# Quantised silu rows of places 3 and 0: absolute value and rounding placed behind the next step's first exponentials; modulations projected ahead of the down product

## The chip, the cores and the metric

The kernel runs on one core of a Trainium2 chip. The time is that of one execution on the device, in microseconds (us); the median of the runs is what is compared. Engines are named as the profile names them: PE is TensorE (matmul, with PEld its weight loads), DVE is VectorE, ACT is ScalarE, POOL is GpSimd, SP is SyncE, which here only issues DMAs.

## The reference

The input x has 16 batches of 512 rows of 256 numbers. Per batch:

```
xn = layernorm(x)
# attention block, 16 heads
q, k   = xn @ cq_w, xn @ ck_w                 # 8 columns a head
qm, km = xn @ qmod_w + b, xn @ kmod_w + b     # the modulations: one number per row and head
scores = causal_kernel(pooled xn)[i - j] + qm[i] + km[j] + 0.15 q.k / sqrt(8),  causal
attn   = softmax(scores);  ctx = attn @ (xn @ v_w + v_b)
h = layernorm(xn + ctx @ out_w + out_b);  s = layernorm(h + gelu(h @ ffn_w1 + b) @ ffn_w2 + b)
# gate block, inputs and weights rounded to FP4 (blocks of 16, E2M1 grid)
hid = silu(fp4(xn) @ fp4(w_gate).T) * (fp4(xn) @ fp4(w_up).T)     # 704 wide
g   = silu(fp4(hid) @ fp4(w_down).T)
out = x + s * g
```

`fp4(t)` divides each block of 16 by its scale (its largest absolute value / 6), rounds to 0, 0.5, 1, 1.5, 2, 3, 4, 6 and multiplies by the scale again. "silu's rows" are the rows of `hid`, which the kernel quantises this way before the product with `w_down` (the down product).

## The kernel before, in words

Everything is laid out as 64 steps: 16 batches times 4 places, g = 0 to 3. Step (b, g) does the attention of heads 4g to 4g + 3 of batch b, and the gate block of the row tile t = g (128 of 512 rows) of batch b. In the same steps the remainder of the batch before (`old` = b - 1) is finished: its output projection in places 0 and 1, its feed-forward block (the contractions `f`) in places 2 and 3. The projections of the batch after (q, k, the modulations m, v) are made by `coming`, partly in places 3, 0 and 1.

A step begins with `context` (32 matmuls into the tile cp: the exponentials of the step before times v), and ct, a copy of cp on ACT. Then the main loop works through a string of letters, `PLAN[g]`:

- W: one burst of scores (PE, tile ws, a pair of PSUM banks with one buffer), their exponential (ACT, tile pr) and POOL's product of that with a table (`tabled`, L560).
- M: the same scores for the *next* step (PE, tile ms, two of six common banks), and `!`: their row maxima (DVE, tile junk, result mx). `!` also runs `caught_up()`, which does deferred work: the low halves of the split projections and their DMAs.
- c: a piece of `coming`; l: a piece of the output projection; x: the turning of quantised inputs xq (PE xqtp, ACT xqT); y: the turning of the quantised hidden rows of the step before (PE hqtp, ACT hqT); k: the copy ct in place 1.

After the letters come the two halves of the hidden rows (PE gp/up/gu, ACT Silu, DVE product into the tile `wide`), the quantisation's first stages, and the down product of the tile of the step before (`gate`: 12 matmuls dp, then ACT Silu into `gated`). `expect(AF.Exp)` loads ACT's table for exponentials and `operands` issues the loads of qT and kT for the step after next (SP, L466 and L467).

The quantisation is a generator, `fp4_stages`, advanced with `next`: DVE finds the largest value amax of each block and its inverse inv, POOL makes the scale (L224) and scales the rows (L222); then ACT writes the scaled absolute value m (the tile m, bf16), DVE does two SCALAR_TENSOR_TENSOR instructions (max with m and add, max and subtract), which round, and POOL multiplies by the scale (L242). With `by_act=False` (in `fp4`, for weights) VectorE took the exponent bits with an AND on 32-bit integers instead, into a float32 tile, and needed two TENSOR_TENSOR behind it.

In the order of PE, DVE and ACT nothing is left to a planner: they execute in the order in which the code issues. POOL's instructions and SP's DMAs are ordered by the framework's scheduler by readiness. In the step before place 0 and place 1 (places 3 and 0), `next(stages)` near the end of the step issues the Abs, and `for _ in stages` at the end of the step the two roundings and L242, so that these come ahead of the next step's first letters on ACT and DVE.

The modulations are written by `split_m`: an Identity on ACT makes the high half, and a deferred `rest` the low half on DVE and four DMAs to q_d or k_d (L393).

Of the kernel before, what the change touches and what calls it, by code (L numbers as in the profile page):

```python
# [11 lines left out]

F32 = mybir.dt.float32
I32 = mybir.dt.int32
F32R = mybir.dt.float32r
BF16 = mybir.dt.bfloat16
AF = mybir.ActivationFunctionType
# [24 lines left out]

ROUND = 12582912.0
TURN = 6.283185
LEVEL = 6291456.0
POWER = 4194304.0
EXPONENT = 0x7F800000
UNDER = 1.0 + 2.0**-22


# [1 line left out]
def tile_block(ctx: ExitStack, tc: tile.TileContext, a: dict, pos: bass.AP, win: bass.AP, out: bass.AP):  # L52
# [140 lines left out]

    v_aug = [keep.tile([P, NT * H * VS + SLOT - VS], F32, name=f"va{i}", tag=f"va{i}") for i in range(2)]

    def fp4_stages(dst, src, n, width, by_act=True):

        nb = width // 16
        widest = 2 * D if width <= 2 * D else I_FF

        def temporary(name, columns):
            return sb.tile([P, widest // columns], F32, name=f"{name}{widest}", tag=f"{name}{widest}")[
                :n, : width // columns
            ]
# [12 lines left out]
        nc.gpsimd.tensor_tensor(blocks(dst), blocks(src), per_block(inv), ALU.mult)  # L222
        if by_act:
            nc.gpsimd.tensor_scalar(scale, amax, -1.0 / 6.0, -1e-12, ALU.mult, ALU.min)  # L224
            yield
            m = sb.tile([P, I_FF], BF16, name="m", tag="m")[:n, :width]
            act.activation(m, dst, AF.Abs, scale=POWER)
            yield
            dve.scalar_tensor_tensor(dst, m, 1.25 * POWER, dst, ALU.max, ALU.add)
            yield  # L230
            dve.scalar_tensor_tensor(dst, m, 1.25 * POWER, dst, ALU.max, ALU.subtract)
        else:
            nc.gpsimd.tensor_scalar(scale, amax, 1.0 / 6.0, 1e-12, ALU.mult, ALU.max)
            yield
            m = sb.tile([P, I_FF], F32, name="m32", tag="pr2")[:n, :width]
            dve.tensor_scalar(m.bitcast(I32), dst.bitcast(I32), EXPONENT, None, ALU.bitwise_and)
            dve.tensor_scalar(m, m, 1.0, LEVEL, ALU.max, ALU.mult)
            yield
            dve.tensor_tensor(dst, dst, m, ALU.add)
            yield  # L240
            dve.tensor_tensor(dst, dst, m, ALU.subtract)
        nc.gpsimd.tensor_tensor(blocks(dst), blocks(dst), per_block(scale), ALU.mult)  # L242

    def fp4(dst, src, n, width):
        for _ in fp4_stages(dst, src, n, width, False):
            pass


# [30 lines left out]
        for image, at in ((q_d[i], own + 2), (k_d[i], own), (k_d[i], own + 4)):  # L279
            nc.sync.dma_start(out=image[:, at : at + 2, :], in_=units)  # L280
    xns, vas, gates = {}, {}, {}
    later = []

    def caught_up():
        while later:
            later.pop(0)()

# [49 lines left out]
    def project(b, x):  # L337
# [44 lines left out]
        def split_m(acc, both, flip, image, at, p0):  # L382
            hi, lo = both[:, 0, :], both[:, 1, :]
            step = slice(None, None, -1) if flip else slice(None)
            act.activation(hi[:, step], acc[:, :P], AF.Identity, bias=m_bias)

            def rest():
                dve.scalar_tensor_tensor(
                    lo[:, step], acc[:, :P], m_bias, hi[:, step].bitcast(F32), ALU.add, ALU.subtract
                )  # L390
                for t in range(NT):
                    to = (NT - 1 - t if flip else t) * P
                    nc.sync.dma_start(  # L393
                        out=image[:, at : at + 2, to : to + P],
                        in_=both[2 * H * t + p0 : 2 * H * t + p0 + H, :, :].bitcast(F32),
                    )

            later.append(rest)
# [315 lines left out]

    HI = I_FF // 2

    def quantised(b, t):

        xq = sb.tile([P, 2, D], F32, name=f"xq_{b}_{t}", tag="xq", bufs=2)
        src = xns[b][t // 2].rearrange("p t d -> p (t d)")  # L720
        return xq, fp4_stages(xq.rearrange("p t d -> p (t d)"), src, P, 2 * D)

    def turned_x(b, t, xq, halves=False):
        xq = xq[:, t % 2, :]
        if halves:
            xqTs[b, t] = sb.tile([P, D], F32, name=f"xqT_{b}_{t}", tag="xqT")
            by_halves(f"xqtp_{b}_{t}", xqTs[b, t], [xq[:, c * P : (c + 1) * P] for c in range(NC)])
            yield 0.21
            return
        tp = bank(f"xqtp_{b}_{t}")  # L730
        for c in range(NC):
            turn(tp[:, c * P : (c + 1) * P], xq[:, c * P : (c + 1) * P])
        xqTs[b, t] = sb.tile([P, D], F32, name=f"xqT_{b}_{t}", tag="xqT")
        act.copy(xqTs[b, t], tp[:, :D])
        yield 0.21

    def hidden(b, t, xqT):

        hid = wide[t % 2]

        def halves():
            for s in range(2):
                cut = slice(s * HI, (s + 1) * HI)
                if s == 1:
                    both = ps_s.tile([P, 2, S], F32, name=f"gu_{b}_{t}", tag="ws")
# [12 lines left out]
                sl = sb.tile([P, HI], F32, name=f"sl_{b}_{t}_{s}", tag="sl", bufs=2)  # L758
                act.activation(sl, gp[:, :HI], AF.Silu)
                dve.tensor_tensor(hid[:, cut], up[:, :HI], sl, ALU.mult)  # L760
                yield

        return hid, halves(), fp4_stages(hid[:, :I_FF], hid[:, :I_FF], P, I_FF)

    def turned_hidden(b, t, hq, halves=False):
        hqT = sb.tile([P, NI, P], F32, name=f"hqT_{b}_{t}", tag="hqT")
# [20 lines left out]
    def expect(function):  # L787
# [8 lines left out]
        ("p|x||yytt|tt", ""),  # L796
    )
    PLAN = (
        "WM!lM!xWcclWM!llWcM!cWllM!y",
        "WM!lkxM!WcclWM!llWccM!llWM!hyy",  # L800
        "WM!fffxM!fWffM!ffhM!ffWffM!fWfffWyy",
        "WM!fffxM!fWiffM!ffWfM!iffWffM!fWffyy",
    )
# [408 lines left out]
    for s in range(STEPS):  # L1212
# [194 lines left out]
```

## Time and profile before

| what | value |
|---|---|
| runs, median (lowest to highest) | 1917.15 us (1915.87 to 1920.88), 3 runs |
| the profiled execution | 1914.35 us, span 1912.6 us |
| busy: PE, DVE, POOL, ACT | 91%, 72%, 68%, 59% of the span |
| mean granted clock of TensorE | 0.94 |
| place 0, steps of batches 2 to 15 | 345.65 us for 14, mean 24.69 |
| place 1, steps of batches 1 to 15 | 482.43 us for 15, mean 32.16 |

The span is cut by the start of `context` into steps. The busy share is an average; a wait counts where TensorE stands still, and the profile names the instruction that ended it. Matmul rows with "x8" are several instructions taken together, and the number behind it in square brackets is the idle time before the row and what ended it. The granted clock is that of TensorE as a share of full speed; while it is 0.5, matmuls take twice as long.

### The profile page before, as it was taken

How to read it: one execution, taken by the hardware profiler on the slowest of the kernel's cores; microseconds unless marked ns; L12 is line 12 of the kernel's file. 1: busy time of each engine (PE TensorE's matmuls, PEld its weight loads, DVE VectorE, ACT ScalarE, POOL GpSimd, SP SyncE). 2: the span in 40 equal slices, each digit the busy share in tenths (PEclk: the TensorE clock that was granted, in tenths of full speed). 3: DMA queues.
4: the chain of work that ended last, by engine and by line, in shares of the span. 5: the costliest groups of instructions: out<-in, count | busy, mean ns of one | idle time of the engine just before them, and what ended most of it. 6: DMA issues, size and time to landing. Idle time of an engine off the chain costs nothing.

```text
span 1912.6 us, 35681 instructions
## 1 busy us (share of the span) xinstructions
PE 1748.2 (91%) x12473; PEld 1276.1 (67%) x12473; DVE 1376.7 (72%) x3736; ACT 1121.6 (59%) x1906; POOL 1304.8 (68%) x1112
## 2 busy tenths in 40 slices
PE   5769799899999989899999989899999989999998
PEld 2234467676776767686777767676776767677666
DVE  5767567877686877778686777877687777777654
ACT  5655456566565656566565656656565656565552
POOL 4467466768586876768585876768586776768571
PEclk8868699999999999999999999999998999998999
DMA  6254242414233242414233242413333242322200
GB/s 201 79 156 129 66 135 72 139 55 125 80 104 118 71 125 73 135 51 127 85 104 118 69 125 75 135 51 113 99 104 114 70 124 79 111 63 89 65 21 12
DMA packets 127223, 184.93 MB, mean 97 GB/s; under 512 B 15410, under 2 KB 57844, under 8 KB 127044
## 3 DMA queue, kind: packets, MB, share of 16 engines
q1 hardware_dynamic: 122544, 181.25, 30.4%
q8 instruction: 99, 1.62, 0.3%
q10 hardware_dynamic: 4052, 0.98, 0.3%
q14 instruction: 80, 0.66, 0.1%
q0 software_dynamic: 448, 0.42, 0.1%
HBM read 136.45 MB, written 45.09 MB: 95 GB/s over the span
## 4 chain that ended last, share of the span: by engine, by line
PE 61%; DVE 16%; ACT 5%; DMA 5%; issue 2%; POOL 1%; SPq 1%; DVEq 0%; ACTq 0%; POOLq 0%
PE f L73 22%; PE dp L73 5%; PE gu L73 5%; PE ws L73 4%; DVE xn L73 4%; PE ms L73 4%; DMA kT<-k_d 4%; PE op L73 4%; DVE junk L73 4%; PE cp L73 4%; PE gp L73 2%; PE up L73 2%; DVE xq L73 2%; PE qk_wq L73 2%; PE vp L73 2%
## 5 line engine op out<-in xcount | busy, mean ns | idle before, releaser
L560 POOL TENSOR_TENSOR pr<-pr,table 128x1024 f32<-128x1024 f32 (+2 forms) x448 | 768.4, 1743 | 124.7 <-ACT pr L73 124.3
L73 DVE CUSTOM_DVE_ANT_0 junk<-ms,mask 128x512 bf16<-128x512 f32 (+3 forms) x1024 | 501.7, 490 | 242.8 <-PE ms L73 173.0
L73 ACT ACTIVATE pr<-ws 128x1024 f32<-128x1024 f32 x320 | 327.7, 1024 | 149.6 <-PE ws L73 148.2
L73 PE MATMUL f<-w,act 64*128 64x256 f32 (+1 forms) x1984 | 282.5, 382 | 0.0
L73 DVE SCALAR_TENSOR_TENSOR wide<-m,wide 128x704 f32<-128x704 bf16 x130 | 131.2, 1010 | 157.1 <-ACT m L73 154.8
L73 ACT ACT_TABLE_LOAD x168 | 215.5, 1283 | 34.9 <-PE gp L73 17.2
L73 PE MATMUL f<-hT,w 128*128 128x256 f32 x1024 | 226.3, 379 | 0.0
L73 PE MATMUL ms<-kT,qT 36*128 36x512 f32 (+3 forms) x1024 | 205.4, 393 | 17.4 <-DMA kT<-k_d 15.7
L242 POOL TENSOR_TENSOR wide<-wide,scale 128x704 f32<-128x704 f32 (+1 forms) x71 | 96.3, 1356 | 177.5 <-DVE wide L73 174.6
L73 PE MATMUL ws<-qT,kT 38*128 38x512 f32 (+3 forms) x1024 | 195.6, 421 | 22.3 <-ACT pr L73 11.4
L73 PEld LDWEIGHTS f<-hT,w 128*128 128x128 f32 x1024 | 194.5, 190 | 26.7 <-ACT hT L73 0.3
L73 PEld LDWEIGHTS f<-w,act 64*128 64x128 f32 (+1 forms) x1984 | 192.3, 186 | 17.1
L73 PE MATMUL dp<-wdT,hqT 128*128 128x256 f32 x768 | 177.4, 381 | 0.0
L73 PEld LDWEIGHTS dp<-wdT,hqT 128*128 128x128 f32 x768 | 145.7, 191 | 27.0
L73 PEld LDWEIGHTS ws<-qT,kT 38*128 38x128 f32 x1024 | 107.1, 205 | 67.5 <-issue 22.9
L73 PE MATMUL cp<-pr,va 128*32 128x512 f32 (+3 forms) x2048 | 151.9, 435 | 0.0
L73 PEld LDWEIGHTS ms<-kT,qT 36*128 36x128 f32 x1024 | 122.2, 204 | 44.4 <-issue 13.7
L73 ACT ACTIVATE act<-f,fb 128x256 f32<-128x256 f32 x256 | 114.8, 471 | 51.0 <-PE f L73 49.2
L73 PEld LDWEIGHTS cp<-pr,va 128*32 128x32 f32 x2048 | 62.1, 110 | 89.7 <-issue 75.0
L222 POOL TENSOR_TENSOR wide<-wide,inv 128x704 f32<-128x704 f32 (+1 forms) x71 | 105.6, 1488 | 23.7 <-DVE inv L73 23.6
L224 POOL TENSOR_SCALAR scale<-amax 128x32 f32<-128x32 f32 (+1 forms) x98 | 39.2, 400 | 109.0 <-DVE amax L73 106.2
L73 ACT ACTIVATE sl<-gu 128x352 f32<-128x352 f32 x64 | 29.6, 463 | 119.1 <-PE gu L73 119.0
(218 smaller groups left out, 3199.0 us busy)
## 6 DMA issues: line engine op xcount, KB each, us to landing
table<-rv SPq DMA_DIRECT2D x64, 1024.0 KB
kT<-k_d SPq DMA_DIRECT2D x256, 76.0 KB
qT<-q_d SPq DMA_DIRECT2D x256, 72.0 KB
x<-in_L_attn_x_dram SPq DMA_DIRECT2D x21, 512.0 KB
q_d<-q_hi SPq DMA_DIRECT2D x32, 256.0 KB
q_d<-q_lo SPq DMA_DIRECT2D x32, 256.0 KB
k_d<-k_hi SPq DMA_DIRECT2D x32, 256.0 KB
k_d<-k_lo SPq DMA_DIRECT2D x32, 256.0 KB
```

Of the source, the lines that this page charges most:

```text
L73: return lambda *args, **kw: self.follow(op(*args, **kw))
L222: nc.gpsimd.tensor_tensor(blocks(dst), blocks(src), per_block(inv), ALU.mult)
L224: nc.gpsimd.tensor_scalar(scale, amax, -1.0 / 6.0, -1e-12, ALU.mult, ALU.min)
L242: nc.gpsimd.tensor_tensor(blocks(dst), blocks(dst), per_block(scale), ALU.mult)
L560: nc.gpsimd.tensor_tensor(part, part, table[:, mine, j * P :], ALU.mult)
```

## The change

Four things:

1. In `fp4_stages` the Abs on ACT is now only chosen with `by_act=True`; the other way makes the same bf16 tile m on DVE (an AND with 0x7FFF on the high 16 bits of each float, then a multiply), and both ways share the two rounding instructions. `by_act` is set for the hidden rows of batches b > 0 and for inputs when there is an `old` batch; in batch 0 and for the weights DVE does it.
2. `PLAN` of places 0 and 1 gets the letters a and z. a advances the stages of the step before by one: the Abs, on ACT behind the first W (in place 1 behind k as well). z does the rest, the two roundings and POOL's L242, behind the second `!`. At the end of places 0 and 3 the stages are left open. x moves behind the second W and its c's.
3. At the end of place 0 the modulations (`coming`, one piece: 16 matmuls qk_m, the two Identities, the two low halves) come ahead of the down product instead of behind it.
4. The DMAs of `split_m` are put in a list `sending` and issued by a `caught_up()` with `send`; `caught_up(False)`, used for the modulations at the end of place 0, leaves them for the next one.

```
-    def fp4_stages(dst, src, n, width, by_act=True):
+    def fp4_stages(dst, src, n, width, by_act=False):
...
+        nc.gpsimd.tensor_scalar(scale, amax, -1.0 / 6.0, -1e-12, ALU.mult, ALU.min)
+        yield
+        m = sb.tile([P, I_FF], BF16, name="m", tag="m")[:n, :width]
         if by_act:
-            nc.gpsimd.tensor_scalar(scale, amax, -1.0 / 6.0, -1e-12, ALU.mult, ALU.min)
-            yield
-            m = sb.tile([P, I_FF], BF16, name="m", tag="m")[:n, :width]
             act.activation(m, dst, AF.Abs, scale=POWER)
-            yield
-            dve.scalar_tensor_tensor(dst, m, 1.25 * POWER, dst, ALU.max, ALU.add)
-            yield
-            dve.scalar_tensor_tensor(dst, m, 1.25 * POWER, dst, ALU.max, ALU.subtract)
         else:
-            nc.gpsimd.tensor_scalar(scale, amax, 1.0 / 6.0, 1e-12, ALU.mult, ALU.max)
-            yield
-            m = sb.tile([P, I_FF], F32, name="m32", tag="pr2")[:n, :width]
-            dve.tensor_scalar(m.bitcast(I32), dst.bitcast(I32), EXPONENT, None, ALU.bitwise_and)
-            dve.tensor_scalar(m, m, 1.0, LEVEL, ALU.max, ALU.mult)
-            yield
-            dve.tensor_tensor(dst, dst, m, ALU.add)
-            yield
-            dve.tensor_tensor(dst, dst, m, ALU.subtract)
+            dve.tensor_scalar(m.bitcast(I16), dst.bitcast(I16)[:, 1::2], 0x7FFF, None, ALU.bitwise_and)
+            dve.tensor_scalar(m, m, POWER, None, ALU.mult)
+        yield
+        dve.scalar_tensor_tensor(dst, m, 1.25 * POWER, dst, ALU.max, ALU.add)
+        yield
+        dve.scalar_tensor_tensor(dst, m, 1.25 * POWER, dst, ALU.max, ALU.subtract)
         nc.gpsimd.tensor_tensor(blocks(dst), blocks(dst), per_block(scale), ALU.mult)
...
-    later = []
-
-    def caught_up():
+    later, sending = [], []
+
+    def caught_up(send=True):
         while later:
             later.pop(0)()
+        while send and sending:
+            sending.pop(0)()
+
+    def whole(pieces):
+        for _ in pieces:
+            pass
+        yield
...
                 dve.scalar_tensor_tensor(
                     lo[:, step], acc[:, :P], m_bias, hi[:, step].bitcast(F32), ALU.add, ALU.subtract
                 )
+                sending.append(send)
+
+            def send():
                 for t in range(NT):
...
-    def quantised(b, t):
+    def quantised(b, t, by_act=False):
...
-        return hid, halves(), fp4_stages(hid[:, :I_FF], hid[:, :I_FF], P, I_FF)
+        return hid, halves(), fp4_stages(hid[:, :I_FF], hid[:, :I_FF], P, I_FF, b > 0)
...
     PLAN = (
-        "WM!lM!xWcclWM!llWcM!cWllM!y",
-        "WM!lkxM!WcclWM!llWccM!llWM!hyy",
+        "WMa!lM!zWccxlWM!llWcM!cWllM!y",
+        "WMka!lM!zWccxlWM!llWccM!llWM!hyy",
...
+                "a": stages,
+                "z": whole(stages),
...
-            xqs[(4 * pair[0] + pair[1]) // 2], more = quantised(*pair)
+            xqs[(4 * pair[0] + pair[1]) // 2], more = quantised(*pair, has_old)
...
+        if has_old and g == 0:
+            for _ in take(coming, 1):
+                caught_up(False)
         if gating:
             gate(*gating, hqTs.pop(gating))
-        if has_old and g == 0:
-            next(coming, None)
         if has_old and g in (1, 2):
             acts[g - 1] = expand(old, g - 1, turned_hs[g - 1], stages)
-        if not has_old or g % 3 == 0:
-            next(stages, None)
...
         if s + 2 < STEPS:
             ahead = operands(*divmod(s + 2, H // 4))
-        for _ in stages:
-            pass
+        if g in (1, 2) or not following:
+            for _ in stages:
+                pass
```

More of the change, by code (lines that the diff above doesn't have):

```diff
@@ L13 @@
 F32 = mybir.dt.float32
-I32 = mybir.dt.int32
+I16 = mybir.dt.int16
 F32R = mybir.dt.float32r
@@ L44 @@
 TURN = 6.283185
-LEVEL = 6291456.0
 POWER = 4194304.0
-EXPONENT = 0x7F800000
 UNDER = 1.0 + 2.0**-22
@@ L222, in fp4_stages @@
         nc.gpsimd.tensor_tensor(blocks(dst), blocks(src), per_block(inv), ALU.mult)
+        nc.gpsimd.tensor_scalar(scale, amax, -1.0 / 6.0, -1e-12, ALU.mult, ALU.min)
+        yield
+        m = sb.tile([P, I_FF], BF16, name="m", tag="m")[:n, :width]
         if by_act:
-            nc.gpsimd.tensor_scalar(scale, amax, -1.0 / 6.0, -1e-12, ALU.mult, ALU.min)
-            yield
-            m = sb.tile([P, I_FF], BF16, name="m", tag="m")[:n, :width]
             act.activation(m, dst, AF.Abs, scale=POWER)
-            yield
-            dve.scalar_tensor_tensor(dst, m, 1.25 * POWER, dst, ALU.max, ALU.add)
-            yield
-            dve.scalar_tensor_tensor(dst, m, 1.25 * POWER, dst, ALU.max, ALU.subtract)
-        else:
-            nc.gpsimd.tensor_scalar(scale, amax, 1.0 / 6.0, 1e-12, ALU.mult, ALU.max)
-            yield
-            m = sb.tile([P, I_FF], F32, name="m32", tag="pr2")[:n, :width]
-            dve.tensor_scalar(m.bitcast(I32), dst.bitcast(I32), EXPONENT, None, ALU.bitwise_and)
-            dve.tensor_scalar(m, m, 1.0, LEVEL, ALU.max, ALU.mult)
-            yield
-            dve.tensor_tensor(dst, dst, m, ALU.add)
-            yield
-            dve.tensor_tensor(dst, dst, m, ALU.subtract)
+        else:
+            dve.tensor_scalar(m.bitcast(I16), dst.bitcast(I16)[:, 1::2], 0x7FFF, None, ALU.bitwise_and)
[4 more added lines that the diff above has]
+        dve.scalar_tensor_tensor(dst, m, 1.25 * POWER, dst, ALU.max, ALU.subtract)
         nc.gpsimd.tensor_tensor(blocks(dst), blocks(dst), per_block(scale), ALU.mult)
     def fp4(dst, src, n, width):
-        for _ in fp4_stages(dst, src, n, width, False):
+        for _ in fp4_stages(dst, src, n, width):
             pass
@@ L715, in tile_block @@
     HI = I_FF // 2
-    def quantised(b, t):
+    def quantised(b, t, by_act=False):
         xq = sb.tile([P, 2, D], F32, name=f"xq_{b}_{t}", tag="xq", bufs=2)
         src = xns[b][t // 2].rearrange("p t d -> p (t d)")
-        return xq, fp4_stages(xq.rearrange("p t d -> p (t d)"), src, P, 2 * D)
+        return xq, fp4_stages(xq.rearrange("p t d -> p (t d)"), src, P, 2 * D, by_act)
     def turned_x(b, t, xq, halves=False):
```

## The prediction

> **What bounds the kernel now.** I read the page first, then the waits of TensorE, then a table of windows, one per step of a place, then the timelines of one step in place 0 (batch 9, from 1103.60 us) and of the start of some steps in place 1. On the page TensorE (PE) has by far the largest share:
>
> ```profile
> PE 1748.2 (91%) x12473; PEld 1276.1 (67%) x12473; DVE 1376.7 (72%) x3736; ACT 1121.6 (59%) x1906; POOL 1304.8 (68%) x1112
> ```
>
> So time can be won only in TensorE's 164 us of idleness or in the stretches where its clock is halved. In the steady state its waits are at the start of the steps of places 0 and 1, and there are none in places 2 and 3. These are the large ones (engine, tile, releaser: us, times, longest):
>
> ```profile
> PE xqtp L73 <- ACT pr L73: 31.4, 15, 2.7
> PE ctp L73 <- ACT ct L73: 22.4, 15, 3.2
> PE ms L73 <- DMA kT<-k_d: 15.7, 24, 5.1
> ```
>
> The first two come from ScalarE (ACT), which does the absolute value, the table load, the copy ct and the first exponential in this order (start, duration):
>
> ```profile
> 1105.26 0.79 ACT L73 ACTIVATE m<-wide 128x704 bf16<-128x704 f32 x1 [1.18 <-DVE xq L73]
> 1106.07 1.28 ACT L73 ACT_TABLE_LOAD   x1
> 1107.47 0.57 ACT L73 COPY ct<-cp 128x512 f32<-128x512 f32 x1
> 1107.94 1.03 ACT L73 ACTIVATE pr<-ws 128x1024 f32<-128x1024 f32 x1
> ```
>
> The change attacks that chain. What decides is what comes next in the same step, on VectorE (DVE) and POOL:
>
> ```profile
> 1106.09 2.28 DVE L73 SCALAR_TENSOR_TENSOR wide<-m,wide 128x704 f32<-128x704 bf16 x2 [0.94 <-ACT m L73]
> 1108.29 0.68 DVE L73 CUSTOM_DVE_ANT_0 junk<-ms,mask 128x512 bf16<-128x512 f32 x1
> ...
> 1113.06 0.56 DVE L73 CUSTOM_DVE_ANT_0 junk<-ms,mask 128x384 bf16<-128x384 f32 x1 [0.54 <-PE ms L73]
> ```
>
> ```profile
> 1114.77 0.62 PEld L73 LDWEIGHTS ms<-kT,qT 36*128 36x128 f32 x4 [0.24 <-DVE mx L73]
> ```
>
> The reader sees VectorE go from the two rounding instructions through the first two pairs of maxima without a pause, and the fourth set of products for maxima (ms) waiting until the third maxima have been read: two banks of qk, two of op and two of ms fill the six. TensorE thus runs at the pace of VectorE at 1114.77, and for the 12.5 us to the step's end (1127.32) it has only one more wait over 0.3 us.
>
> **Place 0, 14 steps (batches 2 to 15).** Removed from the start of the step: one Abs (0.79) and its wait (1.18) on ACT, two roundings (2.28 in this step) on VectorE, POOL's closing product (L242, 1.39). Added: the Abs behind the first exponential, the roundings and L242 behind the second maxima. ACT's part is free: with Silu done near 1104.6 (it is some 0.5 later behind the 16 modulation matmuls), table load 1.28, ready 0.2, ct (when cp ends, 1105.96) and exponential 1 end near 1107.5, the Abs near 1108.3, before the roundings are due.
> VectorE: the first products ms end at 1106.62, so the first maxima start near 1106.7 instead of 1108.29, 1.59 earlier. The block from there to the end of the second maxima is 1112.52 − 1108.29 = 4.23, so it ends near 1110.9. Then the two roundings. If these take p, the third maxima start at 1110.9 + p, against 1113.06 before: break-even is p = 2.16.
> What is p? Alone, one takes 0.89 (two: 1.82 in the trace, at 1131.13). Beside the kernel's POOL product of exponentials with the table (L560, 2.36 us for 1024 columns) the nearest row is this one of batch 0, VectorE's pair against POOL's two:
>
> ```profile
> 145.05 3.81 DVE L73 SCALAR_TENSOR_TENSOR wide<-m,wide 128x704 f32<-128x704 bf16 x2
> ```
>
> ```profile
> 144.97 3.14 POOL L560 TENSOR_TENSOR pr<-pr,table 128x768 f32<-128x768 f32 x2 [1.40 <-ACT pr L73]
> ```
>
> Now the products of place 0 run from 1109.85 to 1121.81 back to back, after the roundings. In the changed step the first can start at 1107.61 (end of L711's addition), and the second, behind exponential 2 (which now has the Abs ahead), covers about 1110.0 to 1112.4: the roundings at 1110.9 fall in the middle of it. So p is bounded by 1.82 (no collision) and by 1.5 (rest of product 2) + 0.89 + 1.82 (a 768-column product between the two) + 0.89 = 5.10. I take 3.81, since that row is the same instruction beside the same POOL instruction. The third maxima are then late by 3.81 − 2.16 = 1.65 us, and ms4, which waited for them already, by as much; from there the step is TensorE's own work: +1.65 × 14 = +23.1 us. The 2 to 2.5 us of early waits do disappear; TensorE just arrives sooner at ms4 and waits there.
> The clock I leave as it is. Two steps of place 0:
>
> ```profile
> 994.96:1020.34 25.38, 22.91 (x184) 14.65 (x186) 19.28 (x55) 13.69 (x21) 18.14 (x13) 0.93 0.46 143
> 1103.60:1127.32 23.72, 21.27 (x184) 14.04 (x187) 19.26 (x55) 13.69 (x21) 18.10 (x13) 1.00 0.50 154
> ```
>
> Columns: window, us, busy PE, PEld, DVE, ACT, POOL with instructions, granted clock, DMA share, GB/s. The same work takes 1.66 more at a mean clock of 0.93 than at 1.00, so half-clock stretches cost as much as the waits. A new wait of 2 to 3 us at ms4 stands in for the old one of about that size.
> [...]
> [...]
>
> **Place 1, 15 steps.** Here the wait of xqtp goes (15 times, 31.4 us in all), and x, the Abs of place 0's rows and the roundings move in the same manner. But the next stop stays:
>
> ```profile
> 1243.95 0.57 PE L73 MATMUL ms<-kT,qT 36*128 36x512 f32 x1 [1.26 <-DMA kT<-k_d]
> ```
>
> The second ms starts 7.2 to 8.1 us after the step's start in all batches, when its kT lands, some 6.5 to 7.2 us after its issue, which the change does not move (SP, L467). So what is won ahead of it is lost there. Behind it, the second maxima end some 2.1 later, then roundings (one before POOL's second product, the other behind it: 0.89 + 2.36 + 0.89 = 4.14; bounds 1.82 and 5.10). Third maxima start near 5.4 after that ms, against 4.3 now (1139.57 − 1135.25); ms4 has 0.2 to 0.9 of that left over. I take +0.5 × 15 = +7.5, bounds 0 (ms4 has slack for all of it) and +1.0 × 15 = +15.
>
> **Other parts.** The modulations (16 matmuls, two Identity of 0.31, two roundings ml of 0.30 each) move from the front of place 1 to the end of place 0, ahead of the down product (12 matmuls): the same TensorE work, zero, with the gated Silu 0.5 later, covered by cp (2.3 us of TensorE). The two ml, 0.61 together, leave VectorE's queue behind the first maxima of place 1, and join it where it is done 2.2 us after the step's start, while the first maxima need 3.1: covered; without cover 0.6 × 15 = 9 us. The eight DMAs of L393 stay held until the first catching-up of place 1 and are issued where SP has nothing else from 1129.12 to 1144.18: zero; POOL's queue gets nothing new but L242 between products, and hqtp, its reader, comes 1118.70, with room for one product: a miss would be 1.8 a step, and is inside the bounds below. Batch 0: ten Abs go to VectorE. Two steps lose a wait on ACT, since there Abs stands ahead of the pooled rows (164.25 and 198.91): −1.3 and −1.7, −3 in all. Two passes for each of ten take about 0.63 each for 704 columns (scaled from 457 ns for 512, the f32 AND now done by VectorE for the weights): 10 × 1.26 = 12.6, off the path as I take it. Bounds: −6.4 (both waits of 3.2 vanish) and −3 + 12.6 = +9.6.
>
> **The sum.** +23.1 + 7.5 − 3 = +27.6 on the profiled execution's 1914.35 (span 1912.6) gives 1942; the median of the runs is 2.8 above that execution: 1945.
>
> **The rivals.**
> *No collision, faster.* L242 or idleness of POOL lies where the roundings go, and p stays near 1.82. Place 0 then gains 0.34 a step, and with the early waits gone the half clock there goes, 24.69 (the mean of its 14 steps, sum 345.65) to 23.74: 0.95. (0.34 + 0.95) × 14 = 18, place 1 nothing, batch 0 −3: 1893 + 2.8 = 1896. For it: half of the steps already show 1.00. Against: POOL is busy for 18 of 24 us, and after 1109.85 without a pause. It decides below p = 2.16.
> *Full collision, much slower.* p = 5.1 in place 0 (+2.94 × 14 = 41) and +15 in place 1, −3: 1967 + 2.8 = 1970. For it: engines that alternate whole instructions on the page's own rows (inv<-amax 128x32 takes 1.69 at 959.95 beside L560, 0.17 alone). Against: the 3.81 row.
> *Does nothing.* p about 2.2 and the waits form again at kT and the banks: 1917. For it: both stops exist now. Against: p has no row near 2.2 under L560.
>
> **How the numbers follow.** Forecast 0.47, no collision 0.25, full collision 0.18, nothing 0.10. Runs here differ by 0.3% (1915.87 to 1920.88), the least that can be told from no change. Faster 0.25, same 0.10, slower 0.65. The range runs from 1894, so that the faster case is in, to 1970; the forecast's own goes from 1926 (p 2.8, place 1 +0.2 a step) to 1959 (p 4.5, place 1 +0.8).
>
> **What the profile after should show.** Steps of place 0 of about 26 us instead of 24.69, of place 1 of about 32.7 instead of 32.16 (sum 482.43 over 15); xqtp waiting on pr gone, ctp on ct near zero, PEld of ms waiting 2 to 3 us on DVE mx; ms on kT at 30 us or more, since TensorE arrives earlier; rounding pairs of about 3.8 us in places 0 and 1 beside L560. I am wrong if those pairs stay under 2.2 us, if ms4 does not wait, or if POOL's scheduler puts L242 and the products so that they miss each other, or if the clock in place 0 becomes 1.00 throughout.

## The result, and the profile after

The changed kernel takes 1925.88 us (median of 5 runs, 1925.0 to 1928.67); the kernel before, beside it, 1915.87 (1912.71 to 1920.88). The ratio is 1.0054, 95% interval 1.0035 to 1.0073: slower by 10 us. The forecast had the sign right and the size at nearly three times that. The profiled execution is 1925.88 with a span of 1924.2.

The page after has the same tale of shares, with 13 us more on TensorE; a mean clock of 0.946 hides that some stretches lost and some gained:

```profile
PE 1760.9 (92%) x12473; PEld 1280.5 (67%) x12473; DVE 1427.1 (74%) x3756; ACT 1115.8 (58%) x1896; POOL 1298.1 (67%) x1112
```

The waits of TensorE (engine, tile, releaser: us, times, longest) are what the change was to alter:

```profile
PE ms L71 <- DVE mx L71: 31.5, 42, 2.0
...
PE ms L71 <- DMA k_d<-ml: 15.4, 12, 1.4
...
PE ms L71 <- DMA kT<-k_d: 13.7, 11, 3.7
...
PE xqtp L71 <- ACT pr L71: 2.8, 3, 1.4
...
PE ctp L71 <- ACT ct L71: 1.7, 1, 1.7
```

(The releaser named for a wait can be wrong. The waits named `k_d<-ml` are in place 1, nearly all at the second matmul of ms2, the second set of products for maxima of a step. Whichever name the wait there has, it ends 5.93 after the issue of the last kT load in the mean of 14 batches, so I count them as waits for kT: 29.1 with those named `kT<-k_d`, 15.7 before.) The two waits on ACT, 31.4 and 22.4 before, are down to 2.8 and 1.7, and in their place stands ms waiting for the maxima, 31.5 (21 of it in place 0), 0.3 before. Where it comes from is seen in a step of place 0 (batch 9, from 1107.73), VectorE first, then POOL, then TensorE's matmuls:

```profile
1110.79 0.69 DVE L71 CUSTOM_DVE_ANT_0 junk<-ms,mask 128x512 bf16<-128x512 f32 x1 [1.36 <-PE ms L71]
...
1114.94 3.17 DVE L71 SCALAR_TENSOR_TENSOR wide<-m,wide 128x704 f32<-128x704 bf16 x2
1118.03 0.55 DVE L71 CUSTOM_DVE_ANT_0 junk<-ms,mask 128x384 bf16<-128x384 f32 x1
```

```profile
1111.75 4.69 POOL L561 TENSOR_TENSOR pr<-pr,table 128x1024 f32<-128x1024 f32 x2 [0.49 <-ACT pr L71]
1118.26 1.39 POOL L233 TENSOR_TENSOR wide<-wide,scale 128x704 f32<-128x704 f32 x1 [1.82 <-DVE wide L71]
1119.60 4.95 POOL L561 TENSOR_TENSOR pr<-pr,table 128x768 f32<-128x768 f32 x4
```

```profile
1118.98 0.44 PE L71 MATMUL ms<-kT,qT 36*128 36x384 f32 x1 [0.95 <-DVE mx L71]
1120.02 0.69 PE L71 MATMUL ms<-kT,qT 36*128 36x384 f32 x2 [0.61 <-DVE mx L71]
```

The first maxima start 3.06 us after the step's start (before: 4.69), the block to the end of the second is as long as before, the two roundings take 3.17, and the third maxima start at 10.30 (before: 9.46). ms4, the fourth set of products for maxima, waits for them, 0.95 and 0.61 in this step. Of the pair only the first instruction met a product of POOL's (2.24); the second ran alone (0.89), because POOL then stood idle for 1.82 us, waiting with its closing product (L233, formerly L242), which its order has ahead of the third product. In place 1 the first rounding runs alone (0.89) and the second beside a whole product of 2.36, which makes it 2.9 to 3.1 and the pair about 3.8 to 4.0; in the same batch:

```profile
1141.47 4.02 DVE L71 SCALAR_TENSOR_TENSOR wide<-m,wide 128x704 f32<-128x704 bf16 x2
1142.39 2.36 POOL L561 TENSOR_TENSOR pr<-pr,table 128x1024 f32<-128x1024 f32 x1 [2.37 <-ACT pr L71]
```

Step by step (means of the profiled executions; windows from one start of context to the next):

| | before | after | all steps |
|---|---|---|---|
| batch 1 begins at | 242.18 | 237.10 | -5.1 |
| place 0, 14 steps of batches 2 to 15 | 24.69 | 25.70 | +14.1 |
| of these at full clock throughout | 23.74 (6 steps) | 24.80 (3 steps) | |
| place 1, 15 steps | 32.16 | 32.33 | +2.5 |
| place 2; place 3 (batches 2 to 15) | 27.93; 22.92 | 27.92; 22.91 | -0.1 |

### The profile page after: what moved, and what is told of

It is laid out like the page before. It is cut to its first block, busy times and chain, and to the rows that moved or that the text cites. A ratio compares the mean times of both kernels' runs of the same rounds, so it can differ in the third digit from the quotient of the medians.

```text
span 1924.2 us, 35672 instructions
## 1 busy us (share of the span) xinstructions
PE 1760.9 (92%) x12473; PEld 1280.5 (67%) x12473; DVE 1427.1 (74%) x3756; ACT 1115.8 (58%) x1896; POOL 1298.1 (67%) x1112
## 4 chain that ended last, share of the span: by engine, by line
PE 68%; DVE 14%; DMA 5%; ACT 2%; issue 1%; SPq 1%; POOL 1%; DVEq 0%; POOLq 0%; ACTq 0%
PE f L71 23%; PE dp L71 7%; PE gu L71 6%; PE cp L71 6%; DVE junk L71 6%; DVE wide L71 4%; PE ms L71 4%; PE ws L71 4%; PE gp L71 3%; PE up L71 3%; DMA kT<-k_d 3%; PE vp L71 2%; PE op L71 2%; PE hqtp L71 2%; DVE xn L71 1%
## 5 line engine op out<-in xcount | busy, mean ns | idle before, releaser
L71 DVE SCALAR_TENSOR_TENSOR wide<-m,wide 128x704 f32<-128x704 bf16 (+1 forms) x142 | 184.7, 1301 | 100.5 <-ACT m L71 98.0
L71 PE MATMUL ms<-kT,qT 36*128 36x512 f32 (+3 forms) x1024 | 199.3, 380 | 62.4 <-DVE mx L71 31.5
L71 ACT ACT_TABLE_LOAD x168 | 215.5, 1283 | 35.6 <-PE gp L71 17.9
L71 PE MATMUL ws<-qT,kT 38*128 38x512 f32 (+3 forms) x1024 | 201.1, 428 | 22.1 <-ACT pr L71 9.2
L233 POOL TENSOR_TENSOR wide<-wide,scale 128x704 f32<-128x704 f32 (+1 forms) x71 | 96.6, 1360 | 161.2 <-DVE wide L71 157.1
L71 PEld LDWEIGHTS ws<-qT,kT 38*128 38x128 f32 x1024 | 113.5, 204 | 72.6 <-ACT pr L71 22.8
```

Source lines behind the costliest of these rows:

```text
L71: return lambda *args, **kw: self.follow(op(*args, **kw))
```

## The experiments

Their medians stand beside runs of the kernel before on the same chip (1915.6 to 1918.6); the ratio to it is given with its interval.

**The parts one by one.** First part 1 alone, on the kernel before (the new `fp4_stages` and its arguments, nothing else).

> The kernel before with part 1 of the change alone (absolute value of batch 0 and of the weights by VectorE). In the changed kernel batch 1 begins 5.1 us earlier (237.10 against 242.18). Theory (that is part 1's work and the rest of the kernel is untouched by it): batch 1 begins 4 to 6 earlier, total 1909 to 1914 beside 1915.9 to 1916.7 before. Rival (the lead comes from the modulations, the placement or the held DMAs): no lead, 1915 to 1919.

1913.27 against 1915.58, ratio 0.9991 (0.9975 to 1.0006); batch 1 begins at 237.80, 4.4 earlier, and the total is not told from no change. That the waits on ACT are what brought this lead is not shown. Ahead of batch 1 TensorE's idle time rose, from 65.6 to 68.7 us (72.5 in the changed kernel), and half clock fell, from 102 to 79 (75). A kernel without part 1 (the one with the table's load later, below) begins batch 1 at 238.48, with 82 us of half clock. Over all traces batch 1 begins at 233.2 to 238.3 with part 1 (13 kernels) and at 238.5 to 242.5 without (5).

Parts 3 and 4 alone, on the kernel before:

```
+        if has_old and g == 0:
+            for _ in take(coming, 1):
+                caught_up(False)
         if gating:
             gate(*gating, hqTs.pop(gating))
-        if has_old and g == 0:
-            next(coming, None)
```

(and `sending`, as in the change.)

> The kernel before with parts 3 and 4 alone (modulations ahead of the down product, their DMAs held). Theory (costs nothing, as forecast; undoing place 0 gave 1936 for the clock's sake): 1913 to 1920, place 0 at full clock 23.7 to 23.8. Rival (this move is what made the kernel with place 0 undone slow, for instance by the gated Silu and the table load coming later): 1924 or more, place 0 at full clock 24.0 or more.

1903.69 against 1915.58, ratio 0.9938 (0.9922 to 0.9955): 12 us faster. Neither theory had that. Place 0 at full clock takes 24.06, 0.32 more than before; place 1 with one half-clock stretch 30.95 instead of 31.84. The waits of ms for kT fall from 15.7:

```profile
PE ms L73 <- DMA kT<-k_d: 6.5, 3, 5.0
```

Part 2 alone, on the kernel before (the two plans, letters a and z, the stages left open in places 3 and 0):

> The kernel before with part 2 alone (letters a and z in places 0 and 1, x moved). Theory (place 0 pays for the pair of roundings): place 0 at full clock 24.6 to 24.9 instead of 23.74, mean 25.4 to 25.9, total 1926 to 1934. Rival (the placement itself is free, and the loss comes from its meeting the other parts): 1914 to 1920.

1942.02, ratio 1.0140 (1.0120 to 1.0159): 26 us slower, more than expected. Place 0 at full clock 24.49, mean 25.32; place 1 33.36. Its waits of ms for kT more than double, since TensorE comes to ms2 earlier and kT lands hardly sooner (the wait at its second matmul ends 6.74 after the last kT load's issue; 6.83 in the kernel before):

```profile
PE ms L73 <- DMA kT<-k_d: 38.7, 24, 4.9
PE ms L73 <- DVE mx L73: 26.4, 39, 2.0
```

And the change without part 2:

> The changed kernel with part 2 taken out (plans, Abs and roundings as before), parts 1, 3 and 4 kept. Theory (the parts add up: -2.4 for part 1, -12 for parts 3 and 4, and part 2 alone makes the changed kernel slower): 1898 to 1905. Rival (part 1 and the clock's phase spoil it, as in the kernel with place 0 undone): 1910 or more.

1899.87 against 1918.55, ratio 0.9906 (0.9892 to 0.9921). This beats both kernels, the one before by 18.7 us and the changed one by 26 to 28 (medians, and 0.9906 against 1.0054). So the 10 us lost are a gain of 14 to 19 from parts 1, 3 and 4 and a loss of 26 to 28 from part 2. Between these two kernels the sums of the steps differ by 11.4 in place 0 and 15.2 in place 1. At the same clock a step of place 0 takes 0.3 to 0.7 more (with one half-clock stretch 25.99 against 25.65, with none 24.80 against 24.09) and one of place 1 0.7 to 1.0 (with two 32.65 against 31.96, with one 31.96 against 30.98). By these rows an estimated 15 to 25 of the 26.6 us are there at equal clock; the rest goes with more half clock.

**What the pair of roundings costs in place 0.** In the changed kernel POOL's second product is left out of place 0, so that those weights lack their table:

```
-                tabled(where, table, k)
+                if not (has_old and g == 0 and k == 1):
+                    tabled(where, table, k)
```

> Changed kernel without POOL's second product of exponentials and table in place 0 (from batch 1 on), so those weights lack the table: the roundings find POOL idle. Theory (price of the pair 3.17 us, of which 1.35 is waiting for that product): pair near 1.8, step at full clock 23.3 to 23.6 instead of 24.80, place 0 mean 24.0 to 24.7, total 1903 to 1913. Rival (the pair is not what sets the step): 1923 to 1928.

1910.57, ratio 0.9975 (0.9960 to 0.9990). The pair now takes 1.81, and the step of place 0 is 23.45 in nearly every batch, without half clock in batches 2 to 14:

```profile
1103.81 1.81 DVE L71 SCALAR_TENSOR_TENSOR wide<-m,wide 128x704 f32<-128x704 bf16 x2
```

```profile
1096.60:1120.05 23.45, 22.05 (x184) 14.49 (x183) 19.26 (x55) 13.87 (x22) 15.39 (x12) 1.00 0.52 160
1120.05:1154.31 34.26, 31.56 (x198) 24.72 (x197) 22.44 (x61) 19.11 (x32) 17.84 (x14) 0.85 0.32 96
```

(Windows: us, then busy time of PE, PEld, DVE, ACT and POOL, granted clock, DMA share, GB/s; the second is place 1.) Then the first rounding alone is left out, on place 3's rows:

```
+        if rounds > 1:
             dve.scalar_tensor_tensor(dst, m, 1.25 * POWER, dst, ALU.max, ALU.add)
```

> Changed kernel without the first of the two rounding instructions on place 3's rows, from batch 1 on. Theory (break-even of what stands between second and third maxima in place 0 is 2.16 us): the one left takes 2.24 beside POOL's product, so place 0 is as in the kernel before, 24.6 to 24.9 and 23.8 at full clock, total 1909 to 1916. Rival (the pair doesn't set the step): 1923 to 1928.

1920.76, ratio 1.0018 (1.0004 to 1.0033). At full clock place 0 is where the theory had it, the total is not:

```profile
1113.83 2.25 DVE L71 SCALAR_TENSOR_TENSOR wide<-m,wide 128x704 f32<-128x704 bf16 x1
```

```profile
1106.62:1130.51 23.89, 22.31 (x184) 14.49 (x183) 19.68 (x54) 13.87 (x22) 17.64 (x13) 1.00 0.50 156
1130.51:1164.66 34.15, 31.52 (x198) 24.70 (x197) 22.43 (x61) 19.11 (x32) 17.84 (x14) 0.85 0.30 96
```

What stands between the second and third maxima (p) and the full-clock step of place 0 go together: 1.81 and 23.45, 2.25 and 23.89, 3.17 and 24.80, and 3.40 and 25.04 in the kernel with x put back, below. One microsecond there is one microsecond of the step, and the step of the kernel before (23.74) corresponds to p = 2.1. These four kernels have the modulations in place 0, which the kernel before has not; they are 0.32 of the step. Part 2 without them has 3.16 and 24.49, which puts the break-even of the pair by itself at 2.4. But of what place 0 won (32 and 28 us over 14 steps) place 1 gave back 14 and 24: it takes 33.24 and 33.96 on average instead of 32.33, with the same idle time (3.0 a step) and more half clock. That needed a reason of its own, below.

**What parts 3 and 4 won.** SP's issues at the start of place 1, in the kernel before and then with parts 3 and 4 alone (start, duration, line, transfer):

```profile
1127.37 0.26 SPq L467 DMA_DIRECT2D kT<-k_d  x1
...
1128.00 0.25 SPq L467 DMA_DIRECT2D kT<-k_d  x1
1128.36 0.76 SPq L523 DMA_DIRECT2D table<-rv  x1
1134.72 1.72 SPq L393 DMA_DIRECT2D q_d<-ml  x4
```

```profile
1121.70 0.26 SPq L472 DMA_DIRECT2D kT<-k_d  x1
...
1122.44 0.25 SPq L472 DMA_DIRECT2D kT<-k_d  x1
1123.31 2.22 SPq L398 DMA_DIRECT2D q_d<-ml  x4
1125.64 3.08 SPq L398 DMA_DIRECT2D k_d<-ml  x4
1128.82 0.38 SPq L528 DMA_DIRECT2D table<-rv  x1
```

Before, the 1 MB load of a later step's table follows the kT loads at once (1.0 us after the step's start at 1127.32). With the modulations made earlier, their eight small DMAs are ready by then, the scheduler puts them first, and the table goes out 6.9 after the start (1121.92). The second products for maxima (the second matmul of ms2) start 6.55 us after the step's start on average instead of 7.59. To have the table's part of that alone, a read of one column of the old table tile was added to the kernel before:

```
                 tabled(where, table, k)
+                if has_old and g == 1 and k == 1:
+                    act.copy(scrap, last_table[:, 0, 0:1])
```

> The kernel before; added is only a copy of one column of place 0's table tile on ACT (about 0.2 us) behind the second exponential of place 1, so that the 1 MB load of the table into that tile can't be issued before it. In SP's order the load then stands behind the eight modulation DMAs, as in the changed kernel and in the one with the modulations alone, and not behind kT's loads; TensorE's and VectorE's orders are those of before. Theory (parts 3 and 4 won 12 us because the table no longer shares the DMA engines with the last kT loads of place 1): second products for maxima in place 1 start at 6.0 to 6.6 instead of 7.2 to 8.1 us, its waits on kT gone, place 1 with one half-clock stretch 30.9 to 31.3 instead of 31.84, total 1901 to 1910. Rival (it is the modulations' new place among the matmuls and VectorE's instructions): 1912 to 1919.

1912.96 against 1918.55, ratio 0.9972 (0.9957 to 0.9986): a gain of some 5 us, not 12, and inside the rival's range. The profiled execution, the slowest of its ten (1920.63), has place 1 no shorter: 32.50 on average against 32.16, and with one half-clock stretch 31.65 (3 steps) where the theory had 30.9 to 31.3. The table now goes behind the modulation DMAs; the second matmul of ms2 starts at 7.13, and waits little:

```profile
1130.30 0.25 SPq L467 DMA_DIRECT2D kT<-k_d  x1
1136.96 1.72 SPq L393 DMA_DIRECT2D q_d<-ml  x4
1138.78 1.76 SPq L393 DMA_DIRECT2D k_d<-ml  x4
1140.65 0.47 SPq L523 DMA_DIRECT2D table<-rv  x1
```

```profile
1137.00 0.76 PE L73 MATMUL ms<-kT,qT 36*128 36x512 f32 x1 [0.19 <-ACT xqT L73]
```

So the table's place is at most 0.45 of the 1.04 us. Another 0.32 may be that place 0 takes that much longer with the modulations ahead, so that the step starts later beside SP's queue; that was not tested, and 0.27 is not accounted for. Next, parts 3 and 4 without the holding (`caught_up()` in place of `caught_up(False)`):

> The kernel with parts 3 and 4 alone, but without the holding: the eight modulation DMAs are issued as soon as their low halves are done, and stand in SP's order ahead of the last two kT loads of place 1. Theory (order on SP's queue decides, and the holding is what keeps the kT loads first): these loads are issued some 3 to 4 us later, second products for maxima at 8.5 to 10.5 us, place 1 33 us or more, total 1920 to 1945. Rival (only the table's place matters, small DMAs do not): place 1 as in the kernel with both, 31.25, total 1901 to 1907.

1977.36, ratio 1.0305 (1.0291 to 1.0319): the direction expected, and much more of it. The small DMAs now stand between the kT loads, and the second matmul of ms2 starts 11.80 after the step's start:

```profile
1163.60 0.42 SPq L472 DMA_DIRECT2D kT<-k_d  x1
...
1166.15 1.72 SPq L398 DMA_DIRECT2D q_d<-ml  x4
1167.98 2.52 SPq L398 DMA_DIRECT2D k_d<-ml  x4
1170.54 0.28 SPq L472 DMA_DIRECT2D kT<-k_d  x1
```

```profile
1174.85 0.76 PE L73 MATMUL ms<-kT,qT 36*128 36x512 f32 x1 [3.81 <-DMA kT<-k_d]
1177.26 0.76 PE L73 MATMUL ms<-kT,qT 36*128 36x512 f32 x1 [1.65 <-DMA kT<-k_d]
```

Place 1 takes 36.71. The holding is worth some 70 us against this order (0.9938 and 1.0305, each to the kernel before). The order on SP's queue is shown to matter by this pair. It does not support the table as the reason why kT lands sooner: here the table goes out 0.35 behind the last kT load, and the wait still ends 5.98 after that load's issue, as in the changed kernel (5.93), where the table is 6 us away. Why kT lands 0.9 sooner after its issue than in the kernel before (6.83) stays open.

**Part 2 in pieces.** In the changed kernel, place 0 undone (x left where the change has it):

```
-        "WMa!lM!zWccxlWM!llWcM!cWllM!y",
+        "WM!lM!WccxlWM!llWcM!cWllM!y",
...
+        if has_old and g == 3:
+            next(stages, None)
...
-        if g in (1, 2) or not following:
+        if g != 0 or not following:
```

> The Abs and the roundings of place 3's rows go back to the end of their step; x, the modulations, place 1 and batch 0 stay as changed. Reference: kernel before 1915.9, changed 1925.9; mean step of place 0 24.69 and 25.70 us, of place 1 32.16 and 32.33. Theory (the pair of roundings between the second and third maxima is what place 0 pays for): place 0 falls back to 24.5 to 24.9, -14 us; place 1 may give back 0 to 0.4 a step, since its kT now lands earlier relative to its start only because place 0 is longer; total 1911 to 1918. Rival (moving x, the modulations and the DMAs costs it, and the pair is hidden): place 0 stays at 25.4 or more, total 1922 or more.

1936.39, ratio 1.0099 (1.0063 to 1.0135): slower, not faster. The theory's total falls, and the rival's range has both the total and place 0. Of what the rival blamed, parts 3 and 4 were shown to gain; x, moved here without the roundings, was not yet priced. Place 0 is 25.76 on average with the early waits of old (ctp on ct 1.34 in batch 9), and place 1 32.86. At one half-clock stretch place 0 is shorter than in the changed kernel, 25.57 against 25.99; but it has more of them, 61 us against 44. Place 1 undone in the same way (`"WM!lkM!WccxlWM!llWccM!llWM!hyy"`, and the Abs and roundings of place 0's rows at the end of their step):

> Only place 1: the Abs and the roundings of place 0's rows go back to the end of their step, the rest as changed. Theory (place 1 gains little and loses little, because its second products for maxima start when kT lands, whichever way the exponentials lie): place 1 31.9 to 32.6 us, total 1921 to 1930. Rival (the early exponentials in place 1 are what brought those products 1.1 us forward and are worth a gain): place 1 33.0 or more, total 1934 or more.

1925.23, ratio 1.0047 (1.0027 to 1.0066), place 1 32.33: in the changed kernel, place 1's piece is worth nothing either way. x put back in both places, a and z kept:

> The changed kernel with x back in its old place (before the second W in place 0, before the second M in place 1), a and z as changed. Theory (x is of no account beside the roundings): place 0 at full clock 24.7 to 25.0, total 1921 to 1932. Rival (moving x behind the second W is itself a loss, the roundings less so): 1918 or less.

1920.53, ratio 1.0013 (0.9999 to 1.0027); place 0 at full clock 25.04, a little more than expected, place 1 31.80. The total lies just outside the theory and not with the rival; it is 5 to 8 us below the changed kernel, all of it in place 1 of the profiled executions, which has 44 us of half clock instead of 78. From the other side, on the kernel without part 2 (1899.87), place 1's piece alone:

> The kernel without part 2 (1899.9) with part 2 in place 1 alone (plan of place 1 as changed, Abs and roundings of place 0's rows behind its first and second bursts); place 0's plan as before, x too. With place 0 undone but x moved it was 1936, with place 1 undone 1925, with both places changed 1926. Theory (place 1's placement costs by itself 0.8 to 1.1 us a step at equal clock, plus half-clock stretches, as read from the kernel with place 0 undone): 1925 to 1940. Rival (it was x's move in place 0 that made that kernel slow): 1898 to 1912.

1953.47, ratio 1.0186 (1.0152 to 1.0220), more than its theory had, and x alone:

> The kernel without part 2 (1899.9) with x alone moved in places 0 and 1, Abs and roundings as before. Theory (x is of small account: TensorE waits for the first exponential in xqtp or does without it): 1895 to 1910. Rival (x's move is the loss of part 2): 1920 or more.

1931.66, ratio 1.0080 (1.0058 to 1.0102): here the rival is right that moving x is a loss by itself. x alone and place 1's piece alone cost 1.8 and 2.8% over that kernel (0.9906), and all together 1.5%; place 0's Abs and roundings alone were not run on it. The pieces do not add, so no share of the loss can be given to a piece. What these kernels have in common is more half clock, counted from the trace's clock records. It does not by itself put the kernels in order: x put back has less of it than the kernel without part 2, and part 2 alone as much as the changed kernel. (The batch period is the time from one batch's place 0 to the next, mean of batches 2 to 14; why it is given in windows of 3.413 us comes below.)

| kernel | median us | half clock in places 0 (14 steps) and 1 (15), us | batch period, in windows of 3.413 us |
|---|---|---|---|
| without part 2 | 1899.87 | 31 + 68 | 31.49 |
| before | 1915.87 | 38 + 78 | 31.62 |
| changed | 1925.88 | 44 + 78 | 31.99 |
| x put back | 1920.53 | 44 + 44 | 31.87 |
| part 2 alone | 1942.02 | 41 + 82 | 32.22 |
| one rounding left out | 1920.76 | 3 + 143 | 31.98 |
| x alone | 1931.66 | 72 + 89 | 32.19 |
| place 0 undone | 1936.39 | 61 + 96 | 32.15 |
| place 1's piece alone | 1953.47 | 82 + 126 | 32.50 |

In place 0 a stretch of 3.4 us of half clock costs 1.6 us in the kernel before (25.34 against 23.74) and 1.2 in the changed one (25.99 against 24.80), where it begins some 12.5 us into the step instead of 6.4 to 7.2.

**The clock.** What half clock does to the matmuls is seen in the changed kernel's profile: four of gp together take 2.71 us at a granted clock of 0.50 (from 1777.24) and 1.35 at 1.00 (from 1179.13). The half-clock stretches are 3.413 us or whole multiples of it (33 of 34 in the trace of the kernel before, 34 of 35 in the changed kernel's; in both the odd one is the last, at the kernel's end), and the periods of 31.98 and 31.99 asked whether the total is held near 32 of them. Two further turns of the down product's loop of matmuls in place 2 (repeated work, the output is the same), in the changed kernel:

```
         dp = bank(f"dp_{b}_{t}")
+        if b > 0 and t == 1:
+            for i in range(2):
+                mm(dp[:, :D], hqT[:, i, :], wdT[:, i, :], start=True, stop=True)
```

> The changed kernel with four more matmul instructions in each place 2 (two loops of the down product twice over, about 0.8 to 0.9 us, output the same). The batch period was 109.19 us in the changed kernel, 109.16 with place 1 undone, 109.16 with one rounding, all 31.98 to 31.99 times 3.413, which is the length of one half-clock stretch; the kernel before had 107.92, 31.62 times. Theory (the period has locked to 32 such windows, and half-clock stretches come or go to keep it there): period 109.1 to 109.4 in spite of the added work, total 1924 to 1931, and the half clock in places 0 and 1 less. Rival (coincidence): period about 110.1, total 1936 to 1942.

1927.06, ratio 1.0061 (1.0043 to 1.0079), as good as the changed kernel itself with 0.87 us of matmuls more in each of 15 batches. Period 31.99. The half clock has left place 0 in batches 2 to 14:

```profile
1109.28:1134.10 24.82, 22.33 (x183) 14.48 (x182) 20.58 (x55) 13.88 (x22) 17.66 (x13) 1.00 0.49 151
1134.10:1165.87 31.77, 28.93 (x197) 22.04 (x196) 22.47 (x61) 18.95 (x32) 17.82 (x14) 0.95 0.34 102
1165.87:1194.66 28.79, 28.79 (x213) 22.69 (x212) 22.54 (x55) 17.71 (x28) 22.17 (x19) 1.00 0.21 65
```

The same matmuls in the kernel without part 2:

> The kernel without part 2 with the same four more matmuls in each place 2 that cost the changed kernel nothing (28.79 instead of 27.92 us a step, 15 steps). Its batch period is 107.48 us, 31.49 windows of 3.413 us, so not a whole number. Theory (the changed kernel's period is held at 32 windows, this one's is free): total 1908 to 1918, 8 to 18 more. Rival (such work is for some other reason free in every version): 1897 to 1904.

1934.25 (runs from 1920.37 to 1940.22), ratio 1.0069 (1.0040 to 1.0098): 13 us of work cost 31 to 34, more than either theory had (20 to 40 over its runs); in the profiled execution, one of the slowest, no step of place 0 in batches 2 to 14 is without half clock (6 of 13 were). And twice the work (four turns) in the changed kernel:

> The changed kernel with twice as many more matmuls in each place 2 (about 1.75 us). With the first 0.87 the half clock was gone from place 0, and place 1 had what it had, so there is 0.95 a batch left in place 1 (32.65 against 31.7) to take up the rest. Theory (held at 32 windows as long as there is half clock to give up): period 109.2 to 109.7, total 1926 to 1934. Rival (the first 0.87 was taken up by chance): 1938 to 1942.

1946.50, ratio 1.0141 (1.0106 to 1.0176), period 32.33, above both ranges. It is not held, then: 26 us of work cost 17 to 21 (by the ratios and by the medians). The theory of a held period falls. What the three show is that a microsecond of work can cost next to nothing or more than two. That this depends on where the waits then lie is argued from what follows; no run moved the waits alone.

How the clock goes with the waits was read from the traces of all 18 kernels, by cutting the steady part (260 to 1840 us) into windows of that length. In them every half-clock stretch begins and ends on a grid of 3.413 us that runs through the whole trace, exact to 4 ns. Counted in these traces, the clock of the next window goes with TensorE's idle time summed within one window of the grid:

| clock in the window | idle in it, us | next window full | next window half |
|---|---|---|---|
| full | under 0.7 | 7026 | 0 |
| full | 0.7 to 1.4 | 166 | 52 |
| full | 1.4 and more | 2 | 370 |
| half | under 0.1 | 396 | 108 |
| half | 0.1 to 0.5 | 26 | 59 |
| half | 0.5 and more | 0 | 108 |

From these counts I estimate that two microseconds of waiting at a step's start are free of the clock where the grid leaves under 0.7 of them in each window (half clock after 0 of 7026 such windows), and cost half-clock time where one window holds 1.4 of them (after 370 of 372). With a batch period near a whole number of windows most batches were met alike (31.98, one rounding left out: place 0 in no batch from 2 to 14, place 1 in every one); with 31.62, as in the kernel before, about every other step of place 0 was hit.

## Why the prediction was wrong

- *"The eight DMAs of L393 ... zero"*, and the modulations' move as "the same TensorE work, zero". This is the step that failed. Done alone these parts gain 12 us: place 1 gives 13.7 and place 0 takes 3.3. I had counted the DMAs' own issue time on an idle SP, and not that SP's order would change and that kT would land sooner after its issue, at 5.93 instead of 6.83. The table's 1 MB load, which now goes behind them, is at most 6 of the 12 us; what the rest comes from is open. It is also where "kT ... some 6.5 to 7.2 us after its issue, which the change does not move" fell: the second matmul of ms2 starts at 6.40 after the step's start instead of 7.59. So place 1, forecast at +7.5, came out at +2.5. For part 2 alone, where the table stays right behind the kT loads, it is at 7.39, little moved, and place 1 does lose, 18 us rather than 7.5.
- *The pair, p = 3.81.* This is the other term that was off, and by the windows the larger: 9 of the 16 us between forecast and profiled execution. The mechanism was right: the early waits go, the pair puts off the third maxima, ms4 waits for them. The term was mis-sized: p is 3.17, since the batch-0 row had two products to meet and here POOL had only one ready. Its next in order was L242, which waits for the pair itself. (That L242 and the products might miss each other stood among my signs of being wrong.) With 3.17 in place of 3.81 my own formula gives +1.01 a step and +14.1; place 0 gained 14.1. The agreement is partly luck: 0.32 a step of it is the modulations' move, so the pair by itself costs 0.7, and its break-even is 2.4 rather than 2.16 (2.1 with the modulations in the step).
- *Both ends of p.* 1.81 appears where POOL's product was taken away; a second collision (5.10) never came. The one rounding of the pair that met a product took 1.35 more than 0.89, and 1.50 were left of that product when it began. The product that the 5.10 had between the two roundings is one that POOL's order did not allow. In place 1 I had 4.14; the pair took 3.8 to 4.0.
- *The clock, left as it is.* In the sum this held: half clock in places 0 and 1 went from 116 to 123 us. But it was not a mix to be left alone: taking pieces of the change out or in moved it to between 89 (x back) and 208 us (place 1's piece alone). At 1.2 to 1.6 us a stretch, as in place 0, that is an estimated 42 to 56 us, where these two totals lie 33 apart.
- *Batch 0, -3.* The start is 5.1 us shorter, inside the bounds; the part alone is -2.3 in the median, which its interval does not tell from nothing. The reason given is not confirmed: ahead of batch 1 TensorE's waits for exponentials fell by 1.8 us, but its idle time as a whole rose by 6.9, and what shrank is half clock, by 27.
- *The sum* had +23.1 + 7.5 - 3; the profiled execution had +14.1 + 2.5 - 5.1, within 0.1 of the span's 11.6. For part 2 alone the forecast of +31 would have been near (26), by luck: place 0 took 8.9 where I had 23.1, and place 1 17.9 where I had 7.5. In place 1 at the same clock the step lost 0.7 to 1.0, where I took 0.5.

## What to carry to other kernels

When work is moved, ask what the queue's order becomes, not only what the moved transfers cost: here eight DMAs of 16 KB, made earlier and held until the urgent loads were out, came with a gain of 12 us, and the same eight put ahead of two urgent loads lost 59. The pair of roundings took 3.17 where POOL had one product ready and 3.81 in the row with two, so read the other engine's order before taking a price from a row with more in flight. And before an experiment's total is read as the price of its edit, compare steps at the same clock: moving x cost 5 to 8 us in one kernel and 32 in another, with 34 and 62 us more of half clock.

## What was not expected of the hardware

- The clock's grid and the counts on it, above: in the traces of these 18 kernels half clock came after 370 of 372 full-clock windows of 3.413 us with 1.4 us or more of idle TensorE and after none of 7026 with less than 0.7, and full clock came back after none of 108 half-clock windows with 0.5 or more. The longest single wait in the window ahead of a half-clock stretch was 0.72 to 1.44 us in the changed kernel's trace (27 stretches of the steady part).
- The same added work, 0.87 us a batch, cost 1 us in one kernel and over 30 (by the medians) in another.
- A VectorE rounding that began while POOL's product was in flight took 2.24 us instead of 0.89, the next one 0.89.
